# Keys of the attention layer made block by block, in segment-major order, as the second Mamba of each entry ends

## The chip, the cores and the metric

The kernel runs on one core of one Trainium2 chip. The metric is the device time of one execution in microseconds (us); the kernel before has a median of 14886.81 us over 3 runs (14871.97 to 14890.47). All arithmetic of the stages told of here is in fp32.

## The reference

The input has 4 entries (B), each with 32 variates, 96 segments and 256 channels: 3072 tokens an entry. Two layers follow each other. `layernorm` below is without scale and shift.

```python
# layer 0: two Mambas, one along the segments, one along the variates
xt = mamba_t(group_norm(x) as [4*32, 96, 256])
xd = mamba_d(xt transposed to [4*96, 32, 256])
x  = x + xd transposed back
# layer 1
t = x as [4, 3072, 256]                       # token = variate*96 + segment
n = layernorm(t)
q, k = n @ Wt, n @ Wx                         # [4, 3072, 32] each
h = tanh(q[:, :, None, :] + k[:, None, :, :] + bh)
a = softmax(sum_u(h * Wa) + ba, axis=-1)      # [4, 3072, 3072]
t = t + a @ n
# then a graph attention over 1048576 edges that yields gates, and four gated experts
t = t + experts(layernorm(t), gates(layernorm(t), edge_index))
```

## The kernel before

**Mamba.** `Layer0.run` emits 64 blocks of 384 tokens in a fixed order: the eight t blocks (along segments) of entry 0, the first t block of entry 1, the eight d blocks (along variates) of entry 0, the other t blocks of entry 1, the first of entry 2, the d blocks of entry 1, and so on; entry 3 has its d blocks directly behind its t blocks. A d block holds 12 segments of all 32 variates, and its end (`Layer0.end`) adds the residual and writes its rows to `x1[b]` in DRAM, three tiles of 128 rows at slots 3, 8 and 11 of the block that follows. Each block is 48 slots; the work of each slot is written out by hand in `front`, `back` and `end`. The first 17 blocks are "lone" (`lead`): nothing runs beside them, they use buffers of their own (`self.ld`, on the right side of SBUF, given back at slot 11 of block 17) and part of their work is put on other engines. PE, ACT (ScalarE), DVE (VectorE) and POOL (GpSimd) execute what is emitted strictly in that order; nearly all DMAs are issued by SP's queue, in order too.

**Attention.** `Attention.units` runs over 3072 columns, 768 for each entry. A column is one `tanh` over all 3072 keys for four queries at once (`th`, line 907), followed by its products with `Wa` (`pe`, line 880). Every eight columns make a unit, whose softmax weights are turned and multiplied with the values (`pr`, `ptw`, `pT`, `pv`). As long as Mamba blocks are emitted, one slot goes with one column. An entry's columns need its keys `krep` [128, 3072] and queries `qsel` [128, 768], two buffers of each.

**Side work.** A list `side` holds generators, taken first come, first served. `beside()` takes one step of the first of them, in about three of four columns; where an entry's keys are missing there is no column, and one step is taken per slot. Two kinds are in it. `Attention.keys(b)` makes keys and queries of an entry, two tiles (256 tokens) at a time: 12 steps of load and statistics (lines 799, 800), a root over all 24 tiles (line 790), then 12 times three steps: normalise (795), turn on PE (809, 810), project and copy out (840, 844, 847). `Attention.after(b, ...)` normalises the attention's output and makes tables for the graph, in four parts (`AFTER`). Keys of entry b are asked for when all its d blocks are written, at slot 11 of the following block; `Attention` itself is made when this happens first, in block 17. `load_values` fetches the rows again as values when an entry's columns begin.

**Expert jobs beside Mamba.** `Beside` computes three half blocks of one expert for entries 0 and 1 in one Mamba block (line 1690 is its Gelu). A job is chosen at slot 31, if the other entry's `krep` buffer is free for the weights (no keys of a later entry asked for), at least 40 columns of the current entry are done, and the input of the job is there (`normed`).

**After Mamba.** `steps` in `whole` goes on beside the columns that are left: the edge lists on DVE (`Edges.sort`, paced at 2.3 us a column), one-hot products, indirect gathers on POOL, and expert units (`Experts.early`) while entry 3's columns run. When the columns are over, `tail` does the rest of the experts, the gates and the sums.

Of the kernel before, what the change touches and what calls it, by code (L numbers as in the profile page):

```python
# [74 lines left out]

class Layer0:
# [8 lines left out]
    def __init__(self, ctx, tc, ident, a, x1):  # L85
        self.nc, self.tc = tc.nc, tc
        self.ident, self.a, self.x1 = ident, a, x1
# [484 lines left out]
    def end(self, blk, lead):  # L572
# [33 lines left out]
        def second(k):  # L606
            def f():
# [8 lines left out]
                else:  # L616
                    s0 = i * ns + k * nq
                    nc.vector.tensor_tensor(v["xr", k], v["xr", k], v["po"][:, :C], ALU.add)
                    nc.sync.dma_start(self.x1[b][:, s0:s0 + nq, :].rearrange("v s c -> s v c"),
# [8 lines left out]
        return jobs  # L628

    def run(self):  # L630
# [33 lines left out]
        left, ending = ({}, {}), {}  # L664
        for n, blk in enumerate(blocks):
# [20 lines left out]
            for slot in range(48):  # L686
# [3 lines left out]
                for part in (left[1], jobs[1], ending, ahead):  # L690
                    for f in part.get(slot, []):
                        f()
                if slot == 12:
# [14 lines left out]
                if self.beside:  # L708
                    self.beside(slot, then is None or then["way"] != blk["way"] == "d")
                done = old["b"] if old and slot == 11 and (old["way"], old["i"]) == ("d", NBLK - 1) else None  # L710
                if done == 0:
                    self.lctx.close()
# [7 lines left out]
        yield blocks[-1]["b"]  # L720
# [3 lines left out]
class Attention:  # L724
# [4 lines left out]
    def __init__(self, ctx, tc, ident, a, x1, x2, xn2T, tab_s, tab_a):  # L729
# [15 lines left out]
        self.wt = load("wt_rep", [P, KC, P], a["wt_rep"].rearrange("(k p) m -> p k m", p=P))  # L745
        self.wx = load("wx_rep", [P, KC, P], a["wx_rep"].rearrange("(k p) m -> p k m", p=P))
        self.bh = load("bh_rep", [P, 1], a["bh_rep"])
# [10 lines left out]
        for q in range(2, P // QU):  # L758
# [3 lines left out]
        self.krep, self.qsel = ([const.tile([P, n], F32, tag=f"{k}{i}", name=f"{k}{i}") for i in range(2)]  # L762
                                for k, n in (("krep", TOK), ("qsel", TOK // R_ATT)))
# [38 lines left out]
    def transposed(self, rows):  # L802
# [3 lines left out]
        for k in range(KC):  # L806
            for i in range(CT):
                c0 = (k * CT + i) * P
                self.nc.tensor.transpose(pt[:, c0:c0 + P], rows[:, i, k * P:(k + 1) * P], self.ident)
        self.nc.vector.tensor_copy(t.rearrange("p k x -> p (k x)"), pt)  # L810
        return t

    def keys(self, b):

        nc, s = self.nc, self.state[b]
        x1 = self.x1[b].rearrange("v s c -> (v s) c")
        mv = s["mv"] = self.rows.tile([P, NT, 2], F32, tag="mv1", name="mv1")
        N = NT // CT
        x = self.tiles_of(x1, 0)
        for j in range(N):  # L820
            ahead = self.tiles_of(x1, (j + 1) % N)
            for i in range(CT):
                self.statistics(mv, j * CT + i, x[:, i, :])
            x = ahead
            yield
        rs = s["rs"] = self.inverse_roots(mv)
        krep, qsel = self.krep[b % 2], self.qsel[b % 2]
        W = CT * P
        for j in range(N):
            ahead = self.tiles_of(x1, j + 1) if j + 1 < N else None  # L830
            for i in range(CT):
                self.normalized(x[:, i, :], x[:, i, :], mv, rs, j * CT + i)
            yield
            xT = self.transposed(x)
            x = ahead
            yield
            pq = self.psum("pq")
            for c0, w in ((0, self.wt), (W, self.wx)):
                for k in range(KC):
                    nc.tensor.matmul(pq[:, c0:c0 + W], w[:, k, :], xT[:, k, :], start=(k == 0),  # L840
                                     stop=(k == KC - 1))
            for r in range(R_ATT):
# [1413 lines left out]
```

## Time and profile before

| | us |
|---|---|
| median of 3 runs | 14886.81 (14871.97 to 14890.47) |
| the profiled execution | 14882.76, span 14880.5 |
| lone blocks, up to the first keys | 0 to 2093 |
| Mamba with attention beside, first to last block | 2093 to 11117 |
| attention without Mamba | 11117 to 13950 |
| tail | 13950 to 14880 |
| first and last `th` start | 2291.2 and 13947.5 |

In these four stretches ACT is busy 995, 8460, 2540 and 245 us, DVE 1692, 6875, 1297 and 592, PE 1382, 6958, 2312 and 803. The mean granted TensorE clock is 0.897.

How to read it: a share over the whole span mixes these stretches. A column of attention takes ACT 2.85 us wherever it stands; what differs is what stands beside it. A windows line gives the stretch, its length, then busy us and (x instructions) of each engine or of the chosen instructions, the granted clock, the DMA engines' busy share, and GB/s. A waits line says which engine and line waited for which, in all, how often, and the longest.

### The profile page before, as it was taken

The numbers are of one execution on the slowest core, as the hardware profiler recorded it, in microseconds if no ns is written. First come the engines' busy times: TensorE is split into PE (matmuls) and PEld (weight loads), VectorE is DVE, ScalarE is ACT, GpSimd is POOL, SyncE is SP. The second block draws the span as 40 slices with busy tenths as digits, with TensorE's granted clock in tenths as the row PEclk, the third lists the DMA queues.
The fourth block names the chain that finished last, engine by engine and source line by source line (L and its number), as shares of the span: only waits on it lengthen the run. The fifth ranks groups of instructions, "written<-read, shape, count | busy, mean of one in ns | idle before, by whom it ended". The sixth has DMA issues, their size and how long they took to land.

```text
span 14880.5 us, 224311 instructions
## 1 busy us (share of the span) xinstructions
PE 11456.2 (77%) x86592; PEld 5164.8 (35%) x86592; DVE 10455.7 (70%) x15307; ACT 12241.6 (82%) x9497; POOL 9093.0 (61%) x7108
## 2 busy tenths in 40 slices
PE   5666756777777768888887777788876788888888
PEld 2333322222222323333333333333332334443466
DVE  7888888777777887777777877577767853321376
ACT  3455538999999979999999899999997889999622
POOL 5777777777777767767777677477760035530272
PEclk8998978888888888899999889999988999999999
DMA  6777764445444444444444444354441000000233
GB/s 208 227 230 233 240 206 144 146 150 155 151 151 155 159 151 149 151 152 153 151 151 158 147 149 151 109 153 150 152 142 47 21 13 15 11 21 21 57 103 122
DMA packets 1215833, 1992.43 MB, mean 134 GB/s; under 512 B 420384, under 2 KB 664480, under 8 KB 1209632
## 3 DMA queue, kind: packets, MB, share of 16 engines
q1 hardware_dynamic: 1184032, 1972.03, 41.9%
q0 software_dynamic: 30720, 5.96, 0.7%
q8 instruction: 681, 11.16, 0.3%
q14 instruction: 400, 3.28, 0.1%
HBM read 1867.39 MB, written 110.18 MB: 133 GB/s over the span
## 4 chain that ended last, share of the span: by engine, by line
PE 19%; ACT 17%; DVE 8%; issue 4%; DMA 1%; POOL 1%; SPq 0%; DVEq 0%; ACTq 0%; POOLq 0%
ACT th L907 12%; PE pe L880 8%; PE pv L986 3%; ACT dA L412 2%; PE po L1778 2%; PE ph L1770 1%; DVE h L450 1%; PE pa L1526 1%; ACT pr L970 1%; PE ptw L977 1%; DVE pair L1190 1%; DVE y L1855 1%; PE pz L519 1%; PE ex L1695 0%; PE pc L1363 0%
## 5 line engine op out<-in xcount | busy, mean ns | idle before, releaser
L907 ACT ACTIVATE th<-krep,qsel 128x3072 f32<-128x3072 f32 x3072 | 8668.4, 2847 | 434.4 <-PE pe L880 416.9
L880 PE MATMUL pe<-th,wa_blk 128*32 128x384 f32 x49152 | 5044.6, 538 | 1593.7 <-ACT pr L970 1363.2
L457 POOL TENSOR_TENSOR h<-h,bC 128x768 f32<-128x768 f32 x2048 | 3763.4, 1838 | 2584.3 <-DVE h L450 2190.1
L450 DVE TENSOR_TENSOR_SCAN h<-dA,dB 128x384 f32<-128x384 f32 x3008 | 2706.4, 941 | 991.3 <-ACT dA L412 718.7
L880 PEld LDWEIGHTS pe<-th,wa_blk 128*32 128x32 f32 x49152 | 1462.6, 116 | 4154.1 <-issue 1969.1
L425 DVE TENSOR_TENSOR dB<-bB,dtu 128x768 f32<-128x768 f32 x1912 | 1810.3, 947 | 170.4 <-ACT dtu L500 137.2
L464 POOL TENSOR_TENSOR h<-h 128x768 f32<-128x768 f32 x752 | 1419.9, 1888 | 53.6
L412 ACT ACTIVATE dA<-dt,t_A 128x380 f32<-128x380 f32 x2048 | 1125.5, 571 | 387.0 <-DVE h L450 298.0
L476 PE MATMUL py<-h,ident 128*128 128x384 f32 x2176 | 942.0, 566 | 497.2 <-POOL h L457 497.0
L412 ACT ACTIVATE dA<-dt,d_A 128x372 f32<-128x372 f32 x2048 | 1101.9, 561 | 147.0 <-DVE h L445 109.7
L986 PE MATMUL pv<-xn,pT 128*32 128x257 f32 x18432 | 1101.8, 387 | 144.4 <-DVE pT L979 143.8
L445 DVE TENSOR_TENSOR_SCAN h<-dA,dB 128x768 f32<-128x768 f32 x544 | 947.9, 1750 | 152.7 <-ACT dA L412 90.3
L1045 POOL TENSOR_SCALAR sf<-sel,f 128x32 f32<-128x32 f32 x384 | 141.2, 391 | 1443.8 <-ACT f L1041 1334.6
L979 DVE COPY pT<-ptw 128x512 f32<-128x512 f32 (+1 forms) x768 | 418.6, 545 | 714.1 <-PE ptw L977 713.4
L986 PEld LDWEIGHTS pv<-xn,pT 128*32 128x32 f32 x18432 | 579.6, 111 | 723.9 <-DVE pT L979 275.0
L466 POOL TENSOR_TENSOR y<-y,h 128x384 f32<-128x384 f32 x752 | 784.4, 1043 | 59.0
L465 POOL TENSOR_TENSOR h<-h 128x384 f32<-128x384 f32 x752 | 781.7, 1039 | 59.0
L476 PEld LDWEIGHTS py<-h,ident 128*128 128x128 f32 x2176 | 425.8, 212 | 976.4 <-POOL h L457 749.8
L963 DVE TENSOR_REDUCE nb<-pe 128x1 f32<-128x768 f32 x384 | 362.0, 943 | 397.4 <-PE pe L880 397.1
L1129 POOL DMA_INDIRECT gd<-tab_a,di x480 | 503.1, 1048 | 161.2 <-issue 158.0
L988 DVE COPY pvs<-pv 128x257 f32<-128x257 f32 x384 | 160.4, 418 | 590.8 <-PE pv L986 589.4
L977 PE MATMUL ptw<-ident,pr 128*128 128x128 f32 x2304 | 469.4, 320 | 130.2 <-DVE pT L979 58.6
(304 smaller groups left out, 15203.6 us busy)
## 6 DMA issues: line engine op xcount, KB each, us to landing
bB<-bc SPq DMA_DIRECT2D x2048, 384.0 KB
bC<-bc SPq DMA_DIRECT2D x2048, 384.0 KB
all<-kept SPq DMA_DIRECT2D x40, 1024.0 KB
x<-x SPq DMA_DIRECT2D x144, 256.0 KB
x<-x SPq DMA_DIRECT2D x192, 128.0 KB
kept<-ko SPq DMA_DIRECT2D x43, 512.0 KB
xt<-xn2T SPq DMA_DIRECT2D x41, 512.0 KB
qsel<-xn2T SPq DMA_DIRECT2D x75, 256.0 KB
```

Of the source, the lines that this page charges most:

```text
L412: nc.scalar.activation(inner(dA[:, s * T:(s + 1) * T] if alone else self.dA[s][:, :T]), inner(blk["dt"][:, e, :]), AF.Exp, scale=blk["w"][ ...
L425: nc.vector.tensor_tensor(dB, blk["bB"].pop(j), z["dtu"].unsqueeze(1).to_broadcast([P, SB, T]), ALU.mult)
L445: nc.vector.tensor_tensor_scan(flat(h), dA[:, :SB * T], flat(dB), 0.0, ALU.mult, ALU.add)
L450: nc.vector.tensor_tensor_scan(h[:, s, :], self.dA[s][:, :T], dB[:, s, :], 0.0, ALU.mult, ALU.add)
L457: nc.gpsimd.tensor_tensor(h, h, blk["bC"].pop(j), ALU.mult)
L464: nc.gpsimd.tensor_tensor(h0, h0, h1, ALU.add)
L465: nc.gpsimd.tensor_tensor(h0[:, 0, :], h0[:, 0, :], h0[:, 1, :], ALU.add)
L466: nc.gpsimd.tensor_tensor(y[e], y[e], h0[:, 0, :], ALU.add)
L476: nc.tensor.matmul(z["py"], self.ident, h[:, s, :], start=(i == 0), stop=(i == DS - 1))
L880: nc.tensor.matmul(pe[q * QU:(q + 1) * QU, j, :KQ // 2], self.wa[:, k, :], th[:, c0:c0 + KQ // 2], start=(k == 0), stop=(k == NK - 1))
L907: nc.scalar.activation(th, s["krep"], AF.Tanh, bias=s["qsel"][:, col:col + 1])
L986: nc.tensor.matmul(pv[q * QU:(q + 1) * QU, :C + 1], pT[:, i, q * QU:(q + 1) * QU], s["xn"][:, q * NK + i, :], start=(i == 0), stop=(i == N ...
```

## The change

A new class `Keys` holds the projections, `krep`, `qsel` and the moments of two entries; it is made at the very start, before the lone blocks, and `Attention` takes it over.

- **Order.** Keys (and the values that belong to them) now stand segment by segment: tile n holds segments 4n to 4n+3 of all variates, which is what a d block's rows are. Queries keep their order: each projected group is copied to strided columns of `qsel`. `load_values` issues 24 DMAs of 128 KB instead of 6 of 512 KB, and keys are loaded one tile per DMA.
- **Entries 1 to 3.** `Attention.keys` is called in three parts (`PARTS`): tiles 0 to 17 when d block 5 is written, 18 to 20 after block 6, 21 to 23 after block 7. Each part has its own statistics, root and projection. With up to two groups the rows are loaded once, with more twice, as before.
- **Entry 0.** For d blocks 0 to 6 the statistics are taken on DVE as the rows are finished (in `end`), and from slot 42 of that block on `rows_keys` takes one step a slot: root, reciprocal and shift, normalise (ACT), and for each of three tiles turn (PE), copy (ACT), project (PE), and bias and four query copies (ACT). It uses the PSUM bank `ex`. Block 7's tiles go through `Attention.keys`.
- **Jobs.** A job may be chosen at slot 31, and at slot 44 where there is none; from column 20 instead of 40; not in d blocks 5 to 7.
- **Lists.** After Mamba the edge lists are taken up once the keys of the last entry are there.

```diff
+NQ4 = P // NV
+PARTS = {5: (0, 18), 6: (18, 21), 7: (21, 24)}
+class Keys:
...
+    def project(self, xT, pq, n, pk):
+        W = n * P
+        for to, w in ((pq, self.wt), (pk, self.wx)):
+            for k in range(KC):
+                self.nc.tensor.matmul(to[:, :W], w[:, k, :], xT[:, k, :W], start=(k == 0),
+                                      stop=(k == KC - 1))
+    def queries(self, b, n0, n, pq, copy):
+        for r in range(R_ATT):
+            rp = slice(r * U_ATT, (r + 1) * U_ATT)
+            copy(self.qsel[b % 2][rp].rearrange("p (v m) -> p v m", m=NT)[:, :, n0:n0 + n],
+                 pq[rp, :n * P].rearrange("p (i r v) -> p v i r", r=R_ATT, v=NV)[:, :, :, r])
...
+                    if alone and i < TOK // T - 1:
+                        blk.setdefault("rows", []).append(v["xr", k])
+                        st = wk.tile([P, 6], F32, tag="kst", name="kst", bufs=2)
+                        nc.vector.bn_stats(st, v["xr", k])
+                        nc.vector.bn_aggr(self.keys.of(b)[0][:, i * (T // P) + k, :], st)
...
+    def rows_keys(self, blk):
+        nc, K = self.nc, self.keys
+        n, n0 = T // P, blk["i"] * (T // P)
+        mv, rs = (t[:, n0:n0 + n] for t in K.of(blk["b"]))
+        v = {}
+        def roots():
+            nc.scalar.activation(rs, mv[:, :, 1], AF.Sqrt, bias=K.eps)
+        def shifts():
+            v["m"] = self.ld.tile([P, n], F32, tag="km", name="km")
+            nc.vector.reciprocal(rs, rs)
+            nc.vector.scalar_tensor_tensor(v["m"], mv[:, :, 0], -1.0, rs, ALU.mult, ALU.mult)
+        def normal():
+            v["x"] = self.ld.tile([P, n, C], F32, tag="kx", name="kx")
+            for k in range(n):
+                nc.scalar.activation(v["x"][:, k, :], blk["rows"][k], AF.Identity,
+                                     bias=v["m"][:, k:k + 1], scale=rs[:, k:k + 1])
+        def turn(k):
+            v["p"] = self.ps_x.tile([P, 512], F32, tag="ex", name="kp")
+            for c in range(KC):
+                nc.tensor.transpose(v["p"][:, c * P:(c + 1) * P], v["x"][:, k, c * P:(c + 1) * P],
+                                    self.ident)
+        def copy(k):
+            v["t"] = self.ld.tile([P, KC, P], F32, tag="kt", name="kt")
+            nc.scalar.copy(v["t"].rearrange("p k x -> p (k x)"), v["p"][:, :KC * P])
+        def project(k):
+            K.project(v["t"], v["p"][:, KC * P:], 1, v["p"][:, (KC + 1) * P:])
+        def keep(k):
+            c0 = (n0 + k) * P
+            nc.scalar.activation(K.krep[blk["b"] % 2][:, c0:c0 + P], v["p"][:, (KC + 1) * P:],
+                                 AF.Identity, bias=K.bh)
+            K.queries(blk["b"], n0 + k, 1, v["p"][:, KC * P:], nc.scalar.copy)
+        return [roots, shifts, normal] + [lambda f=f, k=k: f(k) for k in range(n)
+                                          for f in (turn, copy, project, keep)]
...
+                if slot == 42 and old and "rows" in old:
+                    rows = self.rows_keys(old)
+                if rows:
+                    rows.pop(0)()
...
-                    self.beside(slot, then is None or then["way"] != blk["way"] == "d")
-                done = old["b"] if old and slot == 11 and (old["way"], old["i"]) == ("d", NBLK - 1) else None
+                    self.beside(slot, blk["way"] == "d" and blk["i"] >= min(PARTS))
+                done = (old["b"], old["i"]) if old and slot == 11 and old["way"] == "d" else None
...
+    def rows_of(self, b, n):
+        return self.x1[b][:, n * NQ4:(n + 1) * NQ4, :].rearrange("v s c -> s v c")
-    def keys(self, b):
+    def keys(self, b, t0, t1):
...
+        groups = [(n, min(CT, t1 - n)) for n in range(t0, t1, CT)]
+        few, had = len(groups) <= 2, {}
...
-        for q in range(NJ):
-            self.nc.sync.dma_start(xn[:, q * 4:(q + 1) * 4, :C], src[:, q * 4:(q + 1) * 4, :])
+        for n in range(NT):
+            self.nc.sync.dma_start(xn[:, n, :C], self.rows_of(b, n))
...
-        if (not self.jobs or last or att.asked > att.entry + 1 or att.col < 40
+        if (not self.jobs or last or att.asked > att.entry + 1 or att.col < 20
...
-        if slot == 31:
+        if slot == 31 or slot == 44 and not self.job:
             self.choose(last)
...
-                        att.asked = done + 1
-                        side.append(att.keys(done))
+                        if att and i in PARTS:
+                            att.asked = b + 1
+                            side.append(att.keys(b, *PARTS[i]))
...
-                    while lists and us_v > 0 and len(ed.todo) < 2:
+                    while lists and us_v > 0 and len(ed.todo) < 2 and "krep" in att.state[B - 1]:
```

## The prediction

> **What bounds the kernel now.** I read the page first: engine totals, then the 40 slices.
>
> ```profile
> PE 11456.2 (77%) x86592; PEld 5164.8 (35%) x86592; DVE 10455.7 (70%) x15307; ACT 12241.6 (82%) x9497; POOL 9093.0 (61%) x7108
> ...
> DVE  7888888777777887777777877577767853321376
> ACT  3455538999999979999999899999997889999622
> ...
> L907 ACT ACTIVATE th<-krep,qsel 128x3072 f32<-128x3072 f32 x3072 | 8668.4, 2847 | 434.4 <-PE pe L880 416.9
> ```
>
> No engine is the bound throughout. ACT has four regimes: about half busy in the first six slices (lone Mamba blocks), 90% or more in the middle, dips at slices 15, 23, 31, and a low end (tail). Its work is mostly the 3072 `th` columns of 2.847 us. So I asked the windows for `th` alone; the count is the number of columns started.
>
> ```profile
> 2093.00:2291.00 198.00, 0.00 (x0) 0.61 0.54 173
> 2421.00:2601.00 180.00, 137.17 (x49) 0.87 0.49 150
> 5067.00:5218.00 151.00, 104.08 (x38) 0.88 0.49 159
> 5218.00:5299.00 81.00, 0.00 (x0) 0.67 0.51 165
> 8135.00:8267.00 132.00, 85.03 (x31) 0.87 0.47 155
> 8267.00:8407.00 140.00, 92.03 (x33) 0.89 0.43 140
> 11117.00:11493.00 376.00, 251.12 (x91) 0.84 0.15 47
> 11493.00:12067.00 574.00, 436.88 (x158) 0.90 0.08 27
> 12067.00:13950.00 1883.00, 1709.72 (x616) 0.94 0.08 17
> ```
>
> An instruction that crosses an edge counts in both windows, so I use 48, 88, 156 and 612 columns for the second and the last three. An undisturbed Mamba block runs one column per slot: 180/48 = 3.75 us. Two stretches have no column: 198 us before entry 0 (its keys being made) and 81 us before entry 1. The third dip (8135 to 8407) keeps its columns but at 4.3 us: keys run beside them. Mamba ends at 11117, at column 2216; the other 856 take 2833 us: 4.27 us each with keys(3) and the edge lists, 3.68 with lists, 3.08 after. The tail from 13950 to 14880 has no columns. A column run before 11117 instead of after saves 3.08 us if its slot costs no more than before. For the lone blocks, the window from 1246 to 1800 (five d blocks, 111 us each) by engine, PE, PEld, DVE, ACT, POOL:
>
> ```profile
> 1246.00:1800.00 554.00, 394.26 (x1002) 193.54 (x1000) 472.62 (x446) 283.47 (x510) 422.08 (x261) 0.90 0.77 239
> ```
>
> DVE is busy 473 of 554 us (85%), ACT 283 (51%). Who waited for whom in it (us in total, times, longest):
>
> ```profile
> ACT dtu L500 <- POOL dtus L491: 75.9, 20, 5.7
> ...
> ACT zs L526 <- PE pz L519: 51.5, 20, 5.1
> ...
> DVE dB L425 <- ACT dtu L500: 32.0, 17, 3.4
> DVE h L445 <- ACT dA L412: 29.1, 26, 2.3
> ...
> ACT acc L253 <- PE px L238: 22.5, 14, 3.8
> ACT dbl L298 <- PE pd L291: 19.9, 5, 4.9
> ```
>
> ACT waits 75.9 + 51.5 + 22.5 + 19.9 = 170 us for POOL and PE; DVE waits 32.0 + 29.1 = 61 us for ACT. So roughly 61/170 = 0.36 of a delay on ACT reaches DVE, the fuller engine.
>
> **The change part by part** (against the profiled execution, 14882.8 us with a span of 14880.5; the median 14886.8 is 4 us more).
>
> *Entry 0 starts earlier.* Keys were 12 steps of statistics and 36 of the rest, one per slot: 48 slots in 198 us, 4.1 each. Now blocks 0 to 6 arrive with keys made; the last three tiles are two groups, 2 + 6 = 8 steps, so columns begin 40 slots earlier. 8 x 4.1 + 40 x 3.75 = 183 us instead of 198: -15 us, and 40 columns placed.
>
> *The hole before entry 1.* The 81 us hold 13 `dB` products (32 per 48 slots), so 19 or 20 slots; by the code 19. After: entry 0 ends at slot 20 of block 33; the last keys are asked for at slot 11 and their 8 steps, on the 3 in 4 columns that allow side work, end at about slot 21. One empty slot stays: 18 more columns. In all 58 columns are moved: -58 x 3.08 = -178 us.
>
> *Keys in three parts.* 18 tiles are 9 + 27 steps, then 8 and 8: 52 instead of 48. What 48 cost now: before entry 1, 151 - 38 x 3.75 + 81 - 20 x 3.75 = 15 us; in 8135 to 8407, 272 - 62 x 3.75 = 39 us, all beside columns. After, all are beside columns; I take 35 us an entry, nearer the second: +16 for entries 1 and 2. Of entry 3's steps 44 of 52 move ahead of the Mamba end: +30; the stretch 11117 to 11493 loses them: 376 - 88 x 3.68 = -52, and about 9 columns that now have keys but no lists give +10 back (lists end some 230 columns before the columns do, so the delay itself is hidden; without that room it would cost 9 x 3.08 = 28).
>
> *Table switches.* Each part has its own Sqrt: two more for entries 1 to 3, each a load in, 0.30 us of Sqrt, a load back.
>
> ```profile
> L790 ACT ACT_TABLE_LOAD  x20: 1283/1283/1283, 2137.9 to 13967.7; - x20
> L790 ACT ACTIVATE lrs<-mv,eps x20: 295/302/317, 2139.6 to 13972.3; 128x8 f32<-128x8 f32 x8, 128x24 f32<-128x24 f32 x4, 128x6 f32<-128x6 f32 x4, 128x2 f32<-128x2 f32 x4
> ```
>
> 6 x (1.28 + 0.30 + 1.28) = +17 us, on ACT where it is full. In the lone blocks Sqrt stands right behind the Ln of slot 42, whose set is left anyway: one load more and the Sqrt, 1.6 us x 7 = 11. The rows speak against a further cost: the first load began at 2137.9 and its Sqrt at 2139.6, 0.4 us after the load's end. The Trainium skill (ScalarE: Activation LUTs, What ACT_TABLE_LOAD costs) counts 1283 ns and about 1380 ns of drain for every switch, and its rules say to group by table set, which this change does less. By it, an estimate, 19 switches would cost 26 us more; I go by the rows.
>
> *Lone blocks pay for entry 0's keys.* On DVE, 21 x (0.42 + 0.18) for statistics and 7 x 0.33 for reciprocal and shift: 15 us, all on the path at 85% busy. On ACT per tile: a 256-wide normalise about 0.55, a copy 0.4, a bias 0.4 and four query copies about 0.25 each (estimates between the 384-wide ACT rows, 0.48 to 0.67, and L844's 32x64 copy, 0.22): 2.35 x 21 = 49, with Sqrt's 11 that is 60. Besides, ACT waits twice per tile for PE; queued behind each wait are the decays `dA`, for which DVE's scan waits. `zs` waits 2.6 us a time, behind four 384-wide products; the new groups are a third as wide, so 1 us x 42 = 42. (60 + 42) x 0.36 = 37. Together +52 us. Bounds: +15 (all of ACT's part in its idle half) and 15 + 60 + 42 x 2.6 = +184 (all of it exposed). No gain is possible, as only work is added.
>
> *DMA.* Three parts an entry start with statistics that wait for their rows: L799 waited 17.1 us in 5 cases, so 6 x 3.4 = 20, of which DVE's slack takes half: +10. Values come in 24 issues of about 0.57 us (the strided L586 row) instead of 6 of 0.50: 11 us more of SP, three times beside Mamba; `bB` and `bC` queue behind it, fetched two ahead (three slots, 11 us): +5, between 0 and 25. POOL's queue is passed by nothing.
>
> *Expert jobs.* Both windows in which one may start shift two blocks forward. By the conditions the first is now chosen at slot 44, column 23, of blocks 33 and 49: 13 + 12 = 25, as before (25 Gelus at L1690), so the tail keeps 37 units. Nothing, as long as those two succeed.
>
> Sum: -15 - 178 + 16 + 30 - 52 + 10 + 17 + 52 + 10 + 5 = -105 us. 14882.8 - 105 = 14,778; on the median's footing 14,782.
>
> **Rivals.**
>
> *Everything hidden:* lone blocks at +15, keys beside columns free (0 for 16 + 30), waits free (0 for 15): -105 - 37 - 46 - 15 = -203, 14,684. For it: ACT 51% busy in the lone blocks, and 15 us for keys(1). Against: DVE at 85% there, 39 us for keys(2).
>
> *Slower, by ACT's order:* in the lone blocks each new ACT step waits for PE behind products that wait for POOL, and the decays stand behind it. With 3.8 us a wait (the longest of `acc`'s): 15 + 60 + 160 = 235, +183 on my sum: +78, 14,965. It decides from 52 + 105 = 157 us, 22 us a block, 111 becoming 133. For it: all three engines are coupled in these blocks; against: ACT is idle 49% and the steps stand where no front work is.
>
> *It does not carry through:* the slot-44 jobs fail in both windows: three units to the tail at 930/37 = 25 us, less 2 x 12 (a block with a job takes 192, not 180): +51; and the early experts, with lists beside more of entry 3, finish one pair fewer: +50. Sum -4: 14,883, no change.
>
> **How the numbers follow.** About 0.2% (30 us) is what a measurement can tell here. Forecast 0.58, hidden 0.19, no change 0.10, slower 0.13. Faster by over 0.2%: nearly all of the forecast (0.54), the second, a little of the third: 0.76. Within: 0.11. Slower: 0.13. The range 14,680 to 14,885 takes in the hidden case and the no-change case; the slower case stays out. The forecast's own: 14,710 to 14,860 (lone and keys terms at their ends).
>
> **What would show it.** First `th` near 2093 + 52 + 33 = 2180; lone d blocks 111 to about 118 us; at most two columns missing between entries 0 and 1; Mamba end 115 us later, near 11,232 (-15 + 16 + 17 + 30 + 52 + 15), with some 2274 columns behind it, and 2613 us for the other 798 (2833 - 178 - 52 + 10); 25 Gelus at L1690's place; last column near 13,845 and a tail of 930. Wrong if lone blocks pass 130, if keys beside columns cost over 60 us an entry, or if the tail grows.

## The result and the profile after

The changed kernel takes 14912.30 us (median of 18 runs, 14901.33 to 14929.82), the kernel before beside it 14887.23 (18 runs, 14871.97 to 14897.48): a ratio of 1.0018, 95% interval [1.0011, 1.0025]. The prediction, 14,782 with 14,680 to 14,885, had the direction wrong. The profiled execution took 14908.18 us, its span is 14906.3, the mean granted clock 0.892.

From the page of the changed kernel, the lines that answer to those shown of before; `th` is now at L1019:

```profile
PE 11467.0 (77%) x86704; PEld 5160.6 (35%) x86704; DVE 10420.5 (70%) x15265; ACT 12318.8 (83%) x9676; POOL 9064.7 (61%) x7108
...
DVE  7888887777777777777777777757776784332376
ACT  3445559999999899999998899999998889999622
...
L1019 ACT ACTIVATE th<-krep,qsel 128x3072 f32<-128x3072 f32 x3072 | 8678.6, 2848 | 515.4 <-PE pe L992 496.6
```

Busy time hardly moved (ACT +77 us, DVE -35), and the slices show no new gap; the one number that stands out is that `th` waited 515 us instead of 434. The windows of `th`, as before (stretch, its length, busy us and count, clock, DMA share, GB/s):

```profile
2052.00:2152.00 100.00, 0.00 (x0) 0.67 0.50 155
2435.00:2616.00 181.00, 136.05 (x48) 0.87 0.50 149
4631.00:5273.00 642.00, 413.33 (x149) 0.84 0.46 147
5273.00:6250.00 977.00, 688.55 (x245) 0.90 0.45 146
8055.00:8501.00 446.00, 280.86 (x102) 0.85 0.44 141
11361.00:13975.00 2614.00, 2245.59 (x808) 0.92 0.09 22
```

From the end of the lone blocks to the first `th` it is now 100 us (first line, 2052 to 2152); before it was 261 (2030 to 2291), the last 198 of them with the keys being made. The hole before entry 1 is gone (third line: three blocks with keys beside them, 642 us, 143 columns and one empty slot). (Counts hold the table loads that stand at this line too.) The fourth line is where much of the surplus sits: five blocks with an expert job and no keys, 195.4 us each. In the kernel before, four such blocks:

```profile
5548.00:6312.00 764.00, 549.30 (x196) 0.89 0.46 150
```

191.0 us each, with the same 48 columns. The whole budget follows, cut at the `Ln` of blocks 16, 30 and 50 (slot 42 in a lone block, 43 in the others), where SP comes to the first load of the edge lists, and at the last `th`. The last two columns are versions of the experiments below; all differences are from the profile of before:

| stretch | before, us | predicted | after | e7 | e17 |
|---|---|---|---|---|---|
| lone blocks | 2030 | +52 | +22 | +27 | +25 |
| entry 0 (to block 30) | 2565 | -15 | +14 | +14 | +17 |
| keys(1), entry 1, keys(2) (to block 50) | 3899 | +39 | **+166** | +50 | +12 |
| to the end of Mamba | 2609 | +39 | +56 | +24 | +27 |
| columns that are left | 2845 | -220 | -233 | -245 | -214 |
| tail | 933 | 0 | +1 | +1 | +1 |
| sum | 14880.5 | -105 | +26 | -129 | -132 |

The gain came as forecast. It was paid back in one stretch, between blocks 30 and 50.

### The profile page after: what moved, and what is told of

Same layout as the page of the kernel before. It is cut to its first block, busy times and chain, and to the rows that moved or that the text cites. A ratio compares the mean times of both kernels' runs of the same rounds, so it can differ in the third digit from the quotient of the medians.

```text
span 14906.3 us, 224835 instructions
## 1 busy us (share of the span) xinstructions
PE 11467.0 (77%) x86704; PEld 5160.6 (35%) x86704; DVE 10420.5 (70%) x15265; ACT 12318.8 (83%) x9676; POOL 9064.7 (61%) x7108
## 4 chain that ended last, share of the span: by engine, by line
## 5 line engine op out<-in xcount | busy, mean ns | idle before, releaser
L1019 ACT ACTIVATE th<-krep,qsel 128x3072 f32<-128x3072 f32 x3072 | 8678.6, 2848 | 515.4 <-PE pe L992 496.6
```

What stands on the lines that cost most here:

```text
L1019: nc.scalar.activation(th, s["krep"], AF.Tanh, bias=s["qsel"][:, col:col + 1])
```

## The experiments

**The theory.** A unit is eight columns, a block is 48 slots, and one slot goes with one column, so a unit's steps (the reduce `nb`, the exponential `pr`, the turns `ptw`, the products `pv`) meet the same slots of every block as long as an entry lasts. Where they meet them is fixed by when the entry's columns began. I call the count of columns begun, modulo eight, when a block's `Ln` runs the position (the expectations also say alignment). Read from the traces, before: entry 0 at 0, entries 1 and 2 at 5; after: 0, and 7. The theory: position 7 costs about 5 us in each block with a job. **Rivals:** the jobs themselves cost more where they now stand; the 24 loads of values on SP's queue; the keys in three parts; the place of the keys' buffers, or a lower granted clock. The windows above already speak against the clock: 0.89 in the kernel before at 191.0 us a block, 0.90 in the changed one at 195.4.

The kernel before took 14,995 us on the chip of e1 to e4 and 14,880 to 14,898 on those of the others. The ratios of e1, e3 and e4 therefore flatter the changed kernels and can't be set against 1.0018: that chip costs the kernel before more than them. Behind Mamba e2, the kernel before with shifted columns, took 114 us more than the first profile (some 18 of them for six more columns), e1 and e3 only 12 and 20 more than that of the changed kernel. What is compared is blocks and stretches, and ratios only on like chips.

### Moving the position alone: e1, e2

Two empty slots ahead of entry 1 in the changed kernel (position 5), six in the kernel before (position 7); `pad` starts at 2 or 6:

```diff
-            if b < B and "krep" not in self.state[b]:
+            pad = b == 1 and col == 0 and "krep" in self.state[b] and self.pad > 0
+            self.pad -= pad
+            if b < B and (pad or "krep" not in self.state[b]):
```

> The changed kernel with entry 1's columns begun two slots later (two empty slots), so that the units of eight columns of entries 1 and 2 stand against the slots of the Mamba blocks as in the kernel before (column index modulo 8 at the Ln of slot 43: 5 instead of 7; 2 instead of 4 behind the break of entry 3). In the changed kernel's profile the blocks with an expert job take 195 to 198 us in entry 1's time and 192 to 196 in entry 2's, in the one before 190 to 194 and 189 to 194. Theory 'alignment': the loss comes from where the unit's softmax steps fall in the slots, so these 24 blocks come back to 190 to 193, about 100 us, less 2 x 3 us for two columns: about 14,815. Rival 'place or clock': the keys' buffers lie elsewhere in SBUF, or the granted clock is lower (0.89 against 0.92 in those blocks): they stay at 195 to 198 and the time is 14,915 to 14,920.

Measured: 14809.08 us, ratio 0.9881 [0.9865, 0.9898]. Job blocks of entry 1 (34 to 46 without the two that hold a part of `after`) 191.8 us, of entry 2 (50 to 54) 189.3; the changed kernel has 196.6 and 194.3. Two wasted slots made it faster: its span is 96 us (0.65%) below that of the changed kernel, although its chip is the one that takes longer. The ratios differ by 1.4%, which overstates it for the reason above.

> The kernel before with entry 1's columns begun six slots later, so that the alignment of entries 1 and 2 is that of the changed kernel (7 instead of 5, 4 instead of 2 behind the break). Alignment: the blocks with a job go from 191 to about 196 us, 24 x 4.5 = 110, and six columns more behind Mamba cost 18: about 15,010. Place or clock: the blocks stay at 191 and the time rises by 18 to 25 us, to about 14,910.

Measured: 15112.58 us, ratio 1.0079 [1.0063, 1.0096]. Job blocks of the kernel before (without those that hold a part of `after`) went from 192 us to 198 on the mean (195 to 199), where its position is 7; behind entry 3's break, where it is 4, they stayed at 191. So neither the new keys and the place of their buffers, nor the new jobs, nor the new loads are needed for the loss: the kernel before has it as soon as its columns are shifted.

### The loads of values: e3

```diff
-        for n in range(NT):
-            self.nc.sync.dma_start(xn[:, n, :C], self.rows_of(b, n))
+    def fetch_values(self, b, q):
+        for n in range(q * NT // 6, (q + 1) * NT // 6):
+            self.nc.sync.dma_start(self.state[b]["xn"][:, n, :C], self.rows_of(b, n))
...
+            if b < B and LAG + 2 <= col < LAG + 8:
+                self.fetch_values(b, col - LAG - 2)
```

> The changed kernel with the 24 loads of values issued four at a time over columns 4 to 9 instead of all at column 5. In the changed kernel's profile DVE waited 17.7 and 18.0 us for one bB at the start of entries 1 and 2, and about 14 us in smaller waits at entry 0's. Theory 'queue': the burst on SP's queue holds up the bB and bC loads behind it; spread, the waits fall under 3 us each and the time by 30 to 50 us. Rival: the columns stall there anyway, as in the kernel before (10.5 us in the tanh sequence at the same column), and 10 us or less is gained. A change of a few us may move no column, so alignment stays as it is.

Measured: 14942.18 us, ratio 0.9967 [0.9955, 0.9980] (on the chip of e1 to e4). The waits of DVE from 5150 us on, where entry 1 begins, of the changed kernel (who waited for whom, us in all, times, longest):

```profile
DVE dB L480 <- DMA bB<-bc: 17.7, 1, 17.7
DVE xn L900 <- DMA xn<-x: 6.0, 6, 1.3
```

and with the loads spread:

```profile
DVE xn L900 <- DMA xn<-x: 15.7, 19, 1.4
```

The one wait of 17.7 us is the Mamba's `bB` behind 24 issues on SP's queue. Spread, it is gone, and the values are waited for in small pieces. The pause between two `th` there fell from 19.5 and 19.8 us to 8.5 and 9.2, blocks 33 and 49 from 231 and 233 to 222 and 223. Job blocks stayed at 197: this is a second, separate cost, some 8 to 10 us at each of entries 1 and 2, 18 in all, which lies between the two ranges expected. At entry 0 spreading did not help: `bB` waited 14.9 us in six waits there before the spreading and 14.8 in five with it.

### The keys' steps: e4

```diff
+        if b and t1 < NT:
+            for t in (mv[:, t0:t1, :], rs[:, t0:t1], K.krep[b % 2][:, t0 * P:t1 * P],
+                      K.qsel[b % 2].rearrange("p (v m) -> p v m", m=NT)[:, :, t0:t1]):
+                nc.vector.memset(t, 0.5)
+            for _ in range(4 * len(groups)):
+                yield
+            return
```

> The changed kernel in which parts 1 and 2 of the keys of entries 1 to 3 (tiles 0 to 20) keep their steps but do no work: keys, queries and moments of these tiles are set to a constant instead. In the changed kernel blocks 31 to 34 take 198, 213, 231 and 195 us, 117 over 180 each. Theory 'steps': it is the keys' own DVE and PE work beside full columns, so blocks 31 and 32 fall to 181 to 187 and 33 keeps what comes from its values and last part (about 30); blocks 47 to 49 likewise: 60 to 80 us less for each of entries 1 and 2. Rival 'neighbourhood': d blocks with the after parts and a unit's tail are slow at this alignment whatever the keys do; blocks 31 and 32 stay over 195. Prediction on record had 35 us an entry for the keys.

Measured: 14830.62 us (one run, on the chip of e1 to e4). Blocks 31 to 33 together took 603 instead of 642 us, 47 to 49 609 instead of 653: these 44 of 52 steps cost 39 and 44 us an entry, near the 35 that were predicted. Job blocks were unchanged (195 to 198), so the keys are not the cause.

### The two kernels again, and both cures: e5, e6, e7

> The changed kernel unchanged, on the chip of the next three. Beside the first experiments the kernel before took a median of 14,995 us, beside the changed kernel 14,887: the chips differ. If the difference of chips is common to all kernels, the ratio to the kernel before is again 1.0018 (0.997 to 1.006). If it depends on the kernel (a stretch in which PE is the bound, at a clock that one chip grants and another doesn't), the ratio moves below 1.0, towards the 0.9967 less half a per cent that the run with spread values suggests. Blocks with a job stay at 195 to 198 us.

> The kernel before, for a profile on this chip. Common difference: each stretch (lone blocks, Mamba with attention, attention alone, tail) longer by the same 0.7% on a slow chip, or equal on one like the first. Stretch-dependent: lone blocks 2030 us and blocks with a job 190 to 194 as before, but the attention behind Mamba, 2833 us then, and the tail, 930 then, longer, as in the run with six empty slots (2959 and 948).

> The changed kernel with both edits that helped: entry 1's columns two slots later and values loaded over columns 4 to 9. If the two are independent, the time is that of the two-slot run less the 10 us at each of entries 1 and 2 (the stall of 18 us in the tanh sequence was 9 us with spread values) and some 5 at entry 0: about 20 to 25 us less, ratio about 0.987. If the stall only stood where the alignment's loss would have stood anyway, it gains less than 5.

The changed kernel again: 14924.86 us, ratio 1.0028 [1.0018, 1.0037], job blocks 196.9 and 195.6. The kernel before again: 14883.73 us, its stretches as in its first profile. Two empty slots and spread loads: 14760.40 us, ratio 0.9915 [0.9899, 0.9932], job blocks 190.9 and 189.7. In the budget above its third stretch falls from +166 to +50 us, against +39 predicted. On this one chip e7 against e5 gives what both cures are worth: 164 us, 1.1%.

### Other positions: e8, e15

Four empty slots ahead of entry 1 and two ahead of entry 2 (positions 3, 1, and 6 behind the break); one ahead of entry 1 (6, and 3 behind the break).

> The changed kernel with four empty slots before entry 1 and two more before entry 2: alignment 3 in entry 1's blocks, 1 in entry 2's, 6 behind the break of entry 3 (5 took 188 to 194 us a block with a job, 7 195 to 199, 2 190 to 197). Theory 'alignment': blocks with the same work differ from one alignment to another by some us, each alignment with one value throughout: at least two of the three new ones differ by 3 us. Rival: 7 alone is bad (a unit's Exp falls into slot 14 with the job's Gelu), the three are at 190 to 192.

> One empty slot ahead of entry 1: position 6 for entries 1 and 2, 3 behind entry 3's break. If the loss is a smooth function of the position, job blocks of entries 1 and 2 take 193 to 195 us, between the 190.9 of position 5 and the 196.9 of position 7 (194.9 was seen at 6 behind the break in e8), and those behind the break 192 to 194 as at 3 in e8 (192.8). If only one pair of steps collides at 7, they take 190 to 192 us.

e8: 14933.16 us (one run). Job blocks 193.8 at position 3 (entry 1, without block 34), 193.9 at 1 (51 to 54). Blocks 34 and 50 took 182 us and had no job: with the columns so much later the condition of 20 columns failed at slot 44, both times. Three units of experts more fell to the tail, 160 calls of Gelu there instead of 148, and the tail took 970 us instead of 934: 12 us a unit. That is the prediction's third rival at work, in this kernel and not in the changed one. e15: 14829.37 us (one run). At position 6, 191.3 and 189.0 us, hardly different from 5; behind the break, at 3, 196.1 (192 to 194 were expected), where 4 had 192 in e5 and 193 in the changed kernel's first profile. The loss is not a smooth function of the distance from 7.

### With or without a job: e9, e14, e10

No expert jobs beside Mamba at position 7 (e9) and at 5 (e14); the units that they took fall to the tail. e10 has jobs, at 7, but leaves out their Gelu.

```diff
-        self.jobs = [(b, e, j) for b in range(B - 2) for e in range(NEXP) for j in range(n)]
+        self.jobs = []
```

> The changed kernel without expert jobs beside Mamba (the tail does their 37 units more). In entry 1's and 2's blocks the alignment stays 7 (4 behind the break). Theory 'job against unit': what collides at alignment 7 are the job's steps and the unit's, so that without jobs these blocks take what entry 0's take at alignment 0: 180 to 182 us. Rival 'unit against Mamba': the unit's steps stand badly in the block's own slots, with or without a job: 184 us or more. Where a job is worth 1.5 units of the tail, the time rises by 37 x 25 = 925 us less 25 x 14 = 350, to about 15,500.

> Two empty slots ahead of entry 1 (position 5) and no expert jobs in the Mamba blocks; the expert units that the jobs took are made in the tail instead. At position 7 the blocks without jobs took 185.2 and 185.0 us, against 180.9 us at entry 0's position 0. If the units collide with the Mamba's own slots, blocks at position 5 take 181 to 182 us, and about 3 of the 6 us that a job block loses at position 7 are there without any job. If the loss lies between units and the job's steps alone, they take 184 to 185 us as at position 7.

> The changed kernel whose jobs leave out their Gelu (the products go on with the values before it); alignment 7. Slot by slot the changed kernel loses its 6 us a block against the two-slot run between slots 12 and 26, around the Gelu (slot 14, 2.76 us and two table loads of 1.28, together 5.3). If ACT is simply full, a block falls by 5.3, from 196.5 to about 191. If the collision is of the Gelu with the unit's Exp in the same slot, the loss goes with it: 186 or less. If it is the job's products on PE against the unit's, it falls by less than 5.3: 192 or more.

Blocks 34 to 38 without a job, windows of `th` for e9 and then for e14:

```profile
5271.00:6197.00 926.00, 688.63 (x245) 0.87 0.44 144
```

```profile
5268.00:6173.00 905.00, 686.27 (x245) 0.89 0.45 148
```

185.2 us a block at position 7, 181.0 at position 5, with the same work in them. ACT is busy 896 and 893 us of these windows; what it waited for, e9 first:

```profile
ACT th L1019 <- PE pe L992: 28.0, 33, 2.7
```

```profile
ACT dA L467 <- DVE h L505: 5.7, 10, 1.2
ACT th L1022 <- PE pe L992: 2.8, 5, 0.8
```

ACT is the fullest engine here, so its standstill is what lengthens the block: at position 7 `th` waits 25 us more for `pe` on PE, and the window is 21 us longer. DVE's scan also waits more for the decays `dA` (111 us against 80), but DVE has room (busy 692 of 926 us). In all five blocks of e9 `th` stops at the 14th and at the 38th column behind the `Ln`, together 17.5 of the 28.0 us. The 38th column in block 35, from the timeline, PE first (start, length, instruction, and in brackets what it waited for):

```profile
5590.33 2.79 PE L992 MATMUL pe<-th,wa_blk 128*32 128x384 f32 x16 [1.50 <-ACT pr L1082]
5593.05 4.38 PE L346 MATMUL pd<-xc,t_xproj 128*48 128x384 f32 x8
5597.36 0.66 PE L1089 MATMUL ptw<-ident,pr 128*128 128x128 f32 x4
5597.95 1.50 PE L992 MATMUL pe<-th,wa_blk 128*32 128x384 f32 x16
```

```profile
5593.93 2.84 ACT L1019 ACTIVATE th<-krep,qsel 128x3072 f32<-128x3072 f32 x1
5599.52 2.86 ACT L1019 ACTIVATE th<-krep,qsel 128x3072 f32<-128x3072 f32 x1 [2.74 <-PE pe L992]
```

`pr` takes up the scores of a finished unit; PE waited for it and then does the first `pe` of the next one. Behind that stand the Mamba's product `pd` and the unit's turns `ptw`, and only then the second `pe`, for whose end `th`, which has three buffers, waits 2.7 us. At the 14th column the same happens with the Mamba's product `po` in the place of `pd`, in all five blocks. At position 5 (e14) `po` and `pd` come between two `pe` ahead of `pr` in each of the five blocks, and `th` does not wait at these places.

So of the 6 us a job block loses, some 4 are lost between units and the Mamba's own slots, with no job there; the other 2 need the job. In all e9 took 15124.84 us and e14 15020.21 (one run each). The tail of e9 took 1385 us with 37 units more than the 933 of before: 12 us a unit again, so that the 15,500 expected of e9 was too high. e10 took 14764.87 us (one run), job blocks 190.1 and 188.7: 6.8 us less without a Gelu of 2.76 us and two table loads of 1.28 (5.3 together). That tells little: how much of the 5.3 is hidden at another position was not measured, so the Gelu's own price and the position's are not separated here.

### The job's steps moved instead of the columns: e11

```diff
-    PRODUCTS = {0: (0, 0), 3: (0, 1), 5: (1, 0), 8: (1, 1), 10: (2, 0), 12: (2, 1)}
-    GELU = 14
-    OUTPUTS = {15: (0, 0), 17: (0, 1), 20: (1, 0), 23: (1, 1), 26: (2, 0), 29: (2, 1)}
+    PRODUCTS = {0: (0, 0), 1: (0, 1), 3: (1, 0), 6: (1, 1), 8: (2, 0), 10: (2, 1)}
+    GELU = 12
+    OUTPUTS = {13: (0, 0), 15: (0, 1), 18: (1, 0), 21: (1, 1), 24: (2, 0), 27: (2, 1)}
```

with the loads spread as in e3, position 7 as in the changed kernel.

> The changed kernel with no empty slots, but all of a job's steps except the first product two slots earlier (Gelu in slot 12, outputs from 13 to 27), and values loaded over columns 4 to 9. Job and unit then stand to each other as in the run with two empty slots, while unit and Mamba keep alignment 7. 'Job against unit': blocks with a job at 189 to 193 us, 2 columns more ahead of the Mamba end than there, about 14,755 against 14,885 for the kernel before. 'Unit against Mamba': the blocks stay at 195 to 198, about 14,880.

Measured: 14855.42 us, ratio 0.9977 [0.9968, 0.9987]; job blocks 194.0 and 192.8 instead of 196.9 and 195.6. That is between the two ranges expected: two slots earlier, the job's steps win back 3 of the 6 us, about the share that e9 and e14 leave to the jobs.

### The lone blocks: e12

Statistics on DVE stay, `rows_keys` returns no steps (entry 0's keys, queries and roots are constants, except for the last three tiles).

> The changed kernel whose lone d blocks take the statistics but none of rows_keys' steps (tiles 0 to 20 of entry 0's keys and queries are a constant set at the start). Prediction on record: 52 us for the lone blocks, 15 of them DVE's statistics, 37 from ACT's waits and work. The changed kernel's lone blocks end 20 to 22 us later than before. If DVE's statistics are it, this run ends 13 to 18 later; if ACT's steps are, 2 to 8.

Measured: 14907.06 us (one run). The lone blocks end at 2038 us; in the runs of the changed kernel they end at 2050 to 2057, before at 2030 to 2033. So the statistics cost some 5 to 8 us and the steps of `rows_keys` some 12 to 19, together the 22 of the budget, where 15 and 37 were predicted. It is one run, and the changed kernel's runs differ by 7 us among themselves.

### Taking a slot out: e13, e16, e17

If the position decides, it should not matter whether slots are put in or taken out. In e13 the two statistics steps of entry 1's short last parts share a slot, so that the empty slot before entry 1 goes: position 0 (`b != 1` in the condition below). e16 was meant for entries 1 and 2 (`b == 3`), e17 is exactly these. All three have the loads spread. The edit of e17:

```diff
-            yield
+            if b not in (1, 2) or not few or g:
+                yield
```

> The two statistics steps of entry 1's keys are given in one slot, so that the one empty slot ahead of entry 1 goes: entries 1 and 2 then start their units where entry 0 does (column count 0 modulo 8 at the slot-43 mark of a block), and entry 3 stands at 5; the value loads are spread over six columns as in e3. If what the changed kernel loses in its expert blocks is only where the units fall against the slots, the blocks with an expert job should leave the 196.9 us of the changed kernel; if distance from 7 in either direction is what helps, they take 190 to 192 us as with two empty slots (189.0 to 190.9), and the time is within 25 us of that version's (ratio about 0.990 to 0.993). If it is the earlier position (5) in itself that is good, they take 193 us or more and the ratio is 0.994 to 0.998. If position has nothing to do with it and the two empty slots helped as slack, they stay at 196 to 197 us and the ratio is 0.998 to 1.001.

> As e13, but the two statistics steps are given in one slot for entries 1 and 2, so that no slot is empty ahead of entry 2 either, and both entries stand at position 0 (behind entry 3's break 5). In e13 entry 1's job blocks at position 0 took 187.8 us and entry 2's blocks 50 to 54 at position 7 took 195.5 us. If the position decides, blocks 50 to 54 fall to 187 to 190 us, 30 to 40 us in all, and the time is 14,720 to 14,745 us (ratio 0.989 to 0.991). If entry 2's blocks are slower for another reason (what stands in them), they stay at 194 to 196 us and the time is that of e13, 14,768.

> In e16 the merged statistics were given for entry 0 as well, which moved entry 0 from position 0 to 1; its blocks 18 to 22 took 183.7 us instead of 180.9, and what entry 2 won (blocks 50 to 54: 188.2 instead of 195.5) was lost there. Here the merge is for entries 1 and 2 alone: entries 0, 1 and 2 all at position 0. If the position decides, entry 0's blocks return to 181 us, entry 1's job blocks stay at 188 and entry 2's blocks 50 to 54 at 188, and the time is some 35 to 45 us below that of e13 and e16 on one footing: 14,715 to 14,740 us, ratio 0.988 to 0.990. If the slower entry 0 of e16 had another cause, its blocks stay near 184 us and the ratio near 0.992.

e13: 14768.26 us, ratio 0.9925 [0.9908, 0.9941]. Entry 1's job blocks 187.9 us, at 0. Entry 2 started a column short and stood at 7: its blocks 50 to 54 took 195.5. One kernel, two positions, 8 us apart. e16: 14774.92 us, ratio 0.9922 [0.9906, 0.9939]: no gain over e13, although entry 2's blocks fell to 188.2 as expected. Its condition also held for entry 0, which went from 0 to 1. The windows of `th` show both; first e13 (entry 0's blocks 19 to 22, entry 2's 50 to 54), then e16 in the same blocks:

```profile
2433.00:3157.00 724.00, 547.12 (x194) 0.86 0.46 148
...
8353.00:9330.00 977.00, 688.92 (x245) 0.89 0.44 146
```

```profile
2446.00:3180.00 734.00, 550.05 (x196) 0.87 0.47 146
...
8393.00:9334.00 941.00, 684.24 (x243) 0.91 0.47 152
```

Entry 0 lost 10 us in four blocks (30 in all its blocks), entry 2 won 36 in five. e17 leaves entry 0 alone: 14746.12 us (14741.91 to 14750.92), ratio 0.9906 [0.9890, 0.9923], the fastest of all, 0.9% under the kernel before and 1.1% under the changed one, by the ratios. It lies less far below e13 than expected, 16 us in the spans: entry 2 and the block of the break won 53, some 28 were lost behind the break (position 5 instead of 4) and in the columns after Mamba, and 9 are scattered over the other stretches. Its windows of `th` in blocks 31 to 33, 34 to 38, 47 to 49, and 50 to 54:

```profile
4637.00:5272.00 635.00, 416.28 (x150) 0.85 0.47 149
5272.00:6209.00 937.00, 683.66 (x243) 0.92 0.47 152
7926.00:8361.00 435.00, 279.18 (x101) 0.85 0.46 145
8361.00:9302.00 941.00, 683.69 (x243) 0.91 0.48 152
```

The second line stands against the 977 us that the changed kernel needed for the same five blocks, the last against 972. The waits of the second line's window, changed kernel first:

```profile
DVE h L505 <- ACT dA L467: 90.2, 48, 6.9
DVE pT L1091 <- PE ptw L1089: 51.3, 31, 5.4
...
DVE nb L1075 <- PE pe L992: 40.8, 11, 6.4
ACT th L1019 <- PE pe L992: 36.7, 46, 2.7
```

```profile
DVE h L505 <- ACT dA L467: 98.4, 62, 5.5
...
DVE pT L1096 <- PE ptw L1094: 24.2, 19, 1.7
...
ACT th L1022 <- PE pe L995: 3.0, 9, 0.8
```

In job blocks at position 7 it is again PE that is late: the reduce `nb` waits 40.8 us for `pe` and `th` 36.7; at position 0 `nb` does not wait for it and `th` 3.0. The scan's waits for `dA` are the smaller ones at position 7, and those for the turns (`pT`) don't decide: at position 5 (e7) they are 62.2. With a job `th` stops at the same two columns (13.6 us) and at the 24th and 30th (8.6 and 4.1), where the job's products `ex` also run ahead of `pe`. ACT in blocks 34 to 38, in us:

| run | position | job | length | ACT busy | `th` waits for `pe` |
|---|---|---|---|---|---|
| e14 | 5 | no | 905 | 893 | 2.8 |
| e9 | 7 | no | 926 | 896 | 28.0 |
| e17 | 0 | yes | 937 | 922 | 3.0 |
| e7 | 5 | yes | 946 | 922 | 17.0 |
| e15 | 6 | yes | 948 | 922 | 18.8 |
| changed | 7 | yes | 977 | 925 | 36.7 |

All positions together, mean us of a block (entry 1 / entry 2; blocks with a part of `after` left out):

| position | without job | with job |
|---|---|---|
| 0 | 181 (entry 0) | 187.4 / 188.1 (e17) |
| 1 | 184 (entry 0, e16), 182 (block 50, e8) | 193.9 (e8, entry 2) |
| 3 | 182 (block 34, e8) | 193.8 (e8, entry 1) |
| 5 | 182.1 / 181.0 (e14) | 190.9 / 189.7 (e7) |
| 6 | | 191.3 / 189.0 (e15) |
| 7 | 185.6 / 185.3 (e9) | 196.9 / 195.6 (e5) |

## Why the prediction was wrong, point by point

- **"Nothing, as long as those two succeed"** is the step that failed. The two jobs at slot 44 did succeed, there are 25 as counted, and the blocks that hold them still became 5 to 6 us longer, because the new end of the keys set entries 1 and 2 at position 7 instead of 5. By e5 against e7, in the stretch to block 50: 11 job blocks by 5.9 us, 20 us in the two that also hold a part of `after`, 5 in block 50: 90 us. The prediction counted the starts of the columns to the slot, and let each column moved save 3.08 us "if its slot costs no more than before"; that condition failed, for all the slots behind the shift. With which slots of the Mamba the units would then coincide it did not ask, so the offset stands in its sum at nothing.
- **The values' issues, "+5, between 0 and 25".** Right mechanism, wrong price: `bB` waited 17.7 and 18.0 us where entries 1 and 2 begin, and spreading took 8 and 10 us off these blocks. An issue was priced at 0.57 us after the row of another load; its median is 1.4, and the 24 of entry 1 kept SP busy from 5170 to 5204, 34 us instead of 14:

```profile
L971 SPq DMA_DIRECT2D xn<-x x96: 507/1396/2182, 2112.9 to 11541.7; - x96
```

- **The 58 columns and the 9 without lists.** Right in the sum. 2270 columns had begun where SP comes to the first edge load instead of 2212, and the stretch behind it lost 233 us against 220.
- **Start of entry 0, -15.** It saved 8: 383 us for blocks 17 and 18 with 72 columns, before 391 with 32. The first `th` came at 2152, not near 2180, since the lone blocks took less.
- **The other blocks of entry 0, nothing predicted.** They took 22 us more. 11 are in the two blocks with a part of `after` (193 and 192 us, before 184 and 190); the other ten have 1.1 us each, and the cause of that stays open. One thing did change there: four units share an end (`mx`, `f`, `sf`), and counted modulo 32 instead of 8 entry 0 stood at 0 and 16 before and stands at 8 and 24 now; no run tests this.
- **Lone blocks, +52.** They cost 22. The amounts of work were right, the share that reaches the path was not. Here is what the trace says of the steps of `rows_keys` (min/median/max ns, and who waited):

```profile
L709 ACT ACTIVATE kx<-xr,km,rs x21: 584/585/601, 1368.2 to 2061.5; 128x256 f32<-128x256 f32 x21
...
L127 ACT COPY qsel<-kp x84: 205/227/230, 1380.4 to 2093.0; 32x32 f32<-32x32 f32 x84
...
L720 ACT COPY kt<-kp x21: 363/365/372, 1371.9 to 2083.6; 128x256 f32<-128x256 f32 x21
L727 ACT ACTIVATE krep<-kp,bh_rep x21: 347/367/370, 1380.1 to 2092.0; 128x128 f32<-128x128 f32 x21
...
  ACT krep L727: 42.7, 13
```

0.585 + 0.365 + 0.367 + 4 x 0.227 = 2.23 us a tile (predicted 2.35), and 42.7 us of waiting for PE. That 42 had been predicted is luck: it was 42 waits of 1 us, and there were 13 of 3.3. But 46.8 + 11 + 42.7 = 100 us on ACT gave some 15 at the end of the stretch (e12), 0.15 and not 0.36. The 0.36 took all of DVE's waits for ACT as if all of ACT's waits caused them; ACT's idle half took up most of it instead.

- **Table switches.** Per load and root they cost what the rows said. Of the changed kernel, loads and roots in the lone blocks, with the idle time before them last:

```profile
L699 ACT ACT_TABLE_LOAD x7 | 9.0, 1283 | 0.0
...
L699 ACT ACTIVATE rs<-mv,keps 128x3 f32<-128x3 f32 x7 | 2.1, 297 | 0.1
```

The Trainium skill (ScalarE: Activation LUTs, What ACT_TABLE_LOAD costs) counts a drain of some 1380 ns with each switch; 0.0 and 0.1 us idle in seven cases show none here.

- **Keys, 35 us an entry; first loads, +10; jobs' number, tail 930.** The keys measured 39 and 44. The 35 was chosen between two prices that were misread, 15 and 39: the row from 5067 to 5218 counts 38, but 35 columns began in it (one crossed its edge, two are table loads), and from 8135 to 8407 it was 61 and not 62. So the keys cost 26 and 43 us before. The statistics waited 47.7 us for their rows in all, before 17.1, where 20 more were predicted. 25 jobs, and a tail of 931.
- **The rivals.** None was this one. The slower case had the right sign for another reason: lone blocks at 113 to 115 us, far from 133. The third was priced at 25 us a unit by dividing the whole tail by 37; e8 and e9 measure 12.

With position and loads repaired, e17 gives -132 us on the prediction's own footing, against -105. That is no proof of the sum: position 0 is some 2 to 4 us a job block better than the 5 of the kernel before, which no term holds, and the misses of the lone blocks (-27) and of entry 0 (+32) offset each other.

What stays open: the meeting of `pr`, the Mamba's products and the turns on PE was read in blocks 34 to 38 of entry 1, with and without a job; why 6 is as good as 5, and what 1 and 3 lose with a job, was not followed to the instruction.

## What to carry to other kernels

Where two loops with periods that divide each other share in-order engines, the offset between them is a parameter of the schedule, and any edit that moves the start of one by a slot sets it anew for all the blocks behind it (some 30 here): before pricing the edit, read from the trace at what offset each phase runs and what a block costs there. When a change delivers its counted gain and the total does not move, compare blocks that the change did not touch; a constant surplus in each of them points to the offset, and one or two empty slots are a cheap test. Which waits matter is told by the fullest engine: here the 25 us that ACT's `th` waited, not the longer lists of DVE and POOL. A price for work moved to another stage is the increment (12 us a unit), not the stage's mean (25).

## What was not expected of the hardware

- Twenty-four transfers of 128 KB issued in one go on SP's queue, at 1.4 us an issue, hold up a load that is fetched two ahead for 17.7 and 18.0 us; four at a time, in six columns, they hold it up no more at entries 1 and 2 (e3). At entry 0 waits of up to 5.3 us remain, for a reason that was not looked for.
- The 16 products of one `pe` take 2.79 us right behind PE's wait for `pr` and 1.50 us 7.6 us later, in the timeline of e9 above.
- The kernel before takes 0.7% longer on one chip (14,995 us) than on the four others of the experiments (14,880 to 14,898). In e2, which ran there, Mamba blocks of 180 us still took 180; the columns behind Mamba took 2959 us instead of 2845, with six columns more. Versions of the changed kernel lost less there on the same chip: 2623 and 2631 us (e1, e3) against 2611. What differs between the chips stays open.
